# Two graph layers on one core: a block's degrees taken behind the new group's fields instead of ahead of them

## The chip, the cores and the metric

One Trainium2 chip, one of its cores. The metric is the device time of one execution of the whole kernel, in microseconds (us); lower is better. Stated times are medians over runs.

## What is computed

There are 6250 nodes with 128 features and 206250 directed edges `src -> dst`, sorted by `dst`, each with a type of nine. The reference, cut to what matters (`segsum` adds the rows of the edges that share an index):

```
h   = relu(layernorm(x))
deg = segsum(1, src)                                  # edges that leave a node
h   = relu(segsum((h * max(deg,1)**-0.5)[src], dst))  # first layer
x   = x + h @ W0.T + b0
h   = relu(layernorm(x))
m   = segsum(h[src] @ Wmsg.T + bmsg + embed[type], dst)   # second layer
x   = x + GRU(m, h)
```

The edge list holds every edge in both directions and one loop at each node, so the edges that leave a node are as many as those that reach it. The kernel counts the arriving ones, by type.

## The kernel before

The nodes stand in 49 blocks of 128. The kernel turns the edge list into a dense matrix of edge counts ("adjacency") and then does both layers as matrix products.

*Prologue* (the stage of the change). The edge list is turned and written to a DRAM table `flat`; for each pair of nodes the row of `flat` in which its edges begin is searched (`row_i`). Then a loop of seven passes, `for i in range(NCH)`, goes over seven groups of pairs (six of 4 x 125 pairs, one of 125). Three closures do the work:

- `fetch` gathers a group's edges from `flat` by up to four indirect DMAs on GpSimd's queue (L650) into `got`, which has two buffers. VectorE compares the edges with the pairs (L665, two instructions) and multiplies the comparison into the fields (L672, two). TensorE turns the fields with up to 36 small products (L681). ScalarE copies the three results out of PSUM: `typ` (L691), `code_t` and `lo_t` (L694).
- `count` counts a group's edges by type: five masks on VectorE (`m_dve`, L706), four on ScalarE (`m_act`, L709), nine products and one more on TensorE (L710, L711), two copies on ScalarE into `counts` (L713).
- `degrees` adds up the counts of seven blocks, 896 nodes: seven tiny products on TensorE (L720) into `deg`, which has one PSUM buffer; VectorE makes `scale` out of `deg` (L728) and copies it into `reach` (L731); ScalarE takes the square root of `scale` (L732). The first L732 is preceded by the load of a table for the root.

Then come `rows_of` (reciprocal of the root, L742; shift, L743; seven scaled blocks, L759, on ScalarE as L757 for the last three) and `terms_of` (the float32 rows split into two parts for the products, L763 and L764), which make one of seven pieces of the table `tab1`. In pass i the loop fetches group i, counts group i-1 and makes table piece i-3. Behind the loop the last degrees, counts and rows follow, with the first one-hot tiles (L353).

In the prologue VectorE's instructions stand in the order in which the code issues them (`tc.manual_schedule(engines={DVE})`). The order on TensorE, ScalarE and GpSimd is made by the scheduler; SP's too. Each engine works off its own list in order, so an instruction that waits holds up all that stands behind it.

*First layer.* One-hot tiles are made by VectorE (L353), multiplied on TensorE into adjacency columns (L843), copied out by ScalarE (L855), widened (L947), and multiplied with `tab1` (L811). The adjacency goes to DRAM. *Second layer.* It is read back (L1007), widened by ScalarE (L1011) or VectorE (L1018) and multiplied with the second table; then the GRU (L1061 to L1096). A general path behind a run-time test is not taken for this data.

Of the kernel before, what the change touches and what calls it, by code (L numbers as in the profile page):

```python
# [272 lines left out]
def by_matrix(  # L273
# [117 lines left out]
    with tc.tile_pool(name="pro", bufs=1) as pro, tc.manual_schedule(engines={mybir.EngineType.DVE}):  # L391
# [251 lines left out]
        groups = [(b, min(GB, WB - b)) for b in range(0, WB, GB)]  # L643
        typ_of = {}

        def fetch(b0_, nb):

            got = wnd.tile([P, GB, ROWS, 4, HALF], I16, name="got")
            for b in range(nb):
                nc.gpsimd.indirect_dma_start(  # L650
                    out=got[:, b].rearrange("p r f j -> p (r f j)"),
                    out_offset=None,
                    in_=edges_flat,
                    in_offset=bass.IndirectOffsetOnAxis(ap=row_i[:, b0_ + b : b0_ + b + 1], axis=0),
                )
            typ_of[b0_] = wnd.tile([P, GB * WP], BF16, name="typ")
            w0_ = b0_ * WP
            turns_ = {i: pps.tile([P, 4, P], F32, name="turn") for i in (1, 0, 2)}
            n = nb * ROWS
            g = got[:, :nb].rearrange("p b r f j -> p (b r) f j")  # L660
            inside = first_place[:, 2 * NB * (P - 6) - 2 * GB * ROWS * HALF : 2 * NB * (P - 6)]
            inside = inside.rearrange("p (d a j) -> p d a j", d=2, j=HALF)
            fields = wnd.tile([P, GB * ROWS, 3, 2, HALF], BF16, name="fields")
            for d in range(2):
                nc.vector.tensor_tensor(  # L665
                    inside[:, d, :n].rearrange("p a (j t) -> p a j t", t=2),
                    g[:, :, 0, :].rearrange("p a (j t) -> p a j t", t=2),
                    mine[d][:, b0_ * ROWS : b0_ * ROWS + n].unsqueeze(2).to_broadcast([P, n, HALF // 2, 2]),
                    ALU.is_equal,
                )  # L670
            for d in range(2):
                nc.vector.tensor_tensor(  # L672
                    fields[:, :n, :, d, :],
                    g[:, :, 1:, :],
                    inside[:, d, :n].unsqueeze(2).to_broadcast([P, n, 3, HALF]),
                    ALU.mult,
                )
            for i in (1, 0, 2):
                for b in range(nb):
                    for r in range(ROWS):  # L680
                        nc.tensor.matmul(  # L681
                            turns_[i][:, b, :],
                            fields[:, b * ROWS + r, i].rearrange("p d j -> p (d j)"),
                            ident_b,
                            start=(r == 0),
                            stop=(r == ROWS - 1),
                        )
            for i in (1, 0, 2):
                ws = turns_[i][:, :nb, :WP]
                if i == 1:  # L690
                    nc.scalar.copy(typ_of[b0_][:, : nb * WP].rearrange("j (b p) -> j b p", p=WP), ws)  # L691
                else:
                    to = (code_t, None, lo_t)[i][:, w0_ : w0_ + nb * WP, :]
                    nc.scalar.copy(  # L694
                        to.rearrange("j (b p) t -> j b p t", p=WP), ws.unsqueeze(3).to_broadcast([P, nb, WP, 2])
                    )

        def count(b0_, nb):

            n = nb * WP  # L700
            typ = typ_of.pop(b0_)[:, :n]
            sums_t = tps.tile([P, 512], F32, name="sums")
            for k in range(TYPES):
                if k < first_level:
                    m = wnd.tile([P, GB * WP], BF16, name="m_dve", bufs=6)
                    nc.vector.tensor_scalar(m[:, :n], typ, float(1 + k), None, op0=ALU.is_equal)  # L706
                else:
                    m = wnd.tile([P, GB * WP], BF16, name="m_act", bufs=4)
                    nc.scalar.activation(m[:, :n], typ, AF.Sign, bias=levels[:, k - first_level : k - first_level + 1])  # L709
                nc.tensor.matmul(sums_t[:both, :n], sel[:, k, :], m[:, :n], start=(k == 0), stop=False)  # L710
            nc.tensor.matmul(sums_t[:both, :n], top, ones_b[:1, :n], start=False, stop=True)  # L711
            for d in (0, 1):
                nc.scalar.copy(counts[:, b0_ * WP : b0_ * WP + n, d], sums_t[32 * d : 32 * d + rows3, :n])  # L713

        def degrees(c):
            blocks = slice(c * CB, (c + 1) * CB)
            deg = dps.tile([P, CB], F32, name="deg")
            for k in range(CB):
                w = (c * CB + k) * P // 2
                nc.tensor.matmul(  # L720
                    deg[:, k : k + 1],
                    counts[:TYPES, w : w + P // 2, :].rearrange("t w d -> t (w d)"),
                    ones_b[:, :1],
                    start=True,
                    stop=True,
                )

            nc.vector.scalar_tensor_tensor(  # L728
                scale[:, blocks], deg, 1.0, dev[:, blocks], op0=ALU.max, op1=ALU.mult
            )  # L730
            nc.vector.tensor_copy(reach[:, blocks], deg)  # L731
            nc.scalar.activation(scale[:, blocks], scale[:, blocks], AF.Sqrt)  # L732
# [6 lines left out]
        def rows_of(c):  # L739

            blocks = slice(c * CB, (c + 1) * CB)
            nc.vector.reciprocal(scale[:, blocks], scale[:, blocks])  # L742
            nc.vector.scalar_tensor_tensor(  # L743
                shift_[:, blocks], mean[:, blocks], -0.5, scale[:, blocks], op0=ALU.mult, op1=ALU.mult
            )
            if c < NCH - 2:
                f_of[c] = wnd.tile([P, CB, H], F32, name="f1", bufs=1)
            else:

                place = wnd.tile([P, GB * ROWS, 3, 2, HALF], BF16, name="fields")  # L750
                place = place.rearrange("p a f d j -> p (a f d j)")[:, : 2 * CB * H]
                f_of[c] = place.bitcast(F32).rearrange("p (b f) -> p b f", f=H)
            for k in range(CB):
                b = c * CB + k
                to, of, by, add = f_of[c][:, k, :], xs[:, b, :], scale[:, b : b + 1], shift_[:, b : b + 1]
                if c >= NCH - 3:
                    nc.scalar.activation(to, of, AF.Identity, bias=add, scale=by)  # L757
                else:
                    nc.vector.tensor_scalar(to, of, by, add, op0=ALU.mult, op1=ALU.add)  # L759

        def terms_of(c):
            f, tab = f_of.pop(c), tab1[c]
            nc.vector.tensor_scalar(tab[:, 0], f, 0.0, None, op0=ALU.max)  # L763
            nc.vector.scalar_tensor_tensor(  # L764
                tab[:, 1], f, 0.0, tab[:, 0].bitcast(F32), op0=ALU.max, op1=ALU.subtract
            )

        for i in range(NCH):
            if i >= 3:
                degrees(i - 3)  # L770
            fetch(*groups[i])
            if i >= 1:
                count(*groups[i - 1])
            if i >= 3:
                rows_of(i - 3)
                terms_of(i - 3)
# [366 lines left out]
def gnn_kernel(tc, *args):  # L1143
    with tc.tile_pool(name="bad", bufs=1) as pool:
        bad_i = pool.tile([P, 1], I32, name="bad_i")
        by_matrix(tc, bad_i, *args)
        general(tc, bad_i, *args)
# [47 lines left out]
```

## Time and profile before

| | |
|---|---|
| median of 3 runs | 931.22 us (930.29 to 931.83) |
| the profiled execution | 934.99 us |
| its span, first to last instruction | 933.20 us |
| granted TensorE clock over the span | 0.96 of full |
| TensorE busy | 852.5 us, 91% |
| VectorE busy | 799.1 us, 86% |
| ScalarE busy | 712.3 us, 76% |
| GpSimd busy | 54.6 us, 6% |
| first fetch issued on GpSimd | 31.27 us |
| first fields on VectorE (L665) | 38.58 us |
| first one-hot tile (L353) | 97.28 us |
| first adjacency products that go on without a break (L843) | 113.56 us |

Times of instructions count from the span's start. A timeline row has the start, the time taken, engine, line, operation, output and input with their shapes, how many instructions were merged into the row, and in brackets the engine's idle time before it with what ended it. A row of waits has the waiter, what it waited for, the sum, the number of times and the longest. Ends of TensorE's instructions are modelled, and consecutive instructions of an engine overlap a little, so starts are the safer readings.

### The profile page before, as it was taken

How to read it: one execution, taken by the hardware profiler on the slowest of the kernel's cores; microseconds unless marked ns; L12 is line 12 of the kernel's file. 1: busy time of each engine (PE TensorE's matmuls, PEld its weight loads, DVE VectorE, ACT ScalarE, POOL GpSimd, SP SyncE). 2: the span in 40 equal slices, each digit the busy share in tenths (PEclk: the TensorE clock that was granted, in tenths of full speed). 3: DMA queues.
4: the chain of work that ended last, by engine and by line, in shares of the span. 5: the costliest groups of instructions: out<-in, count | busy, mean ns of one | idle time of the engine just before them, and what ended most of it. 6: DMA issues, size and time to landing. Idle time of an engine off the chain costs nothing.

```text
span 933.2 us, 24704 instructions
## 1 busy us (share of the span) xinstructions
PE 852.5 (91%) x10859; PEld 717.7 (77%) x10859; DVE 799.1 (86%) x835; ACT 712.3 (76%) x1205; POOL 54.6 (6%) x103
## 2 busy tenths in 40 slices
PE   3566499999998999999999979999999999999995
PEld 3354399998997999899999979776777777777775
DVE  5869999999999999999999768998888888877754
ACT  2277898999898899899999984776667676675752
POOL 4561000000000000000000000000000000000000
PEclk9579699999999999999999989999999999999998
DMA  9430177787787689678688798776777667766640
GB/s 283 126 105 32 40 185 238 221 264 232 221 263 233 186 250 276 191 235 273 203 244 274 216 313 289 257 267 211 279 281 243 234 239 264 266 216 225 212 128 23
DMA packets 205664, 203.72 MB, mean 218 GB/s; under 512 B 11178, under 2 KB 190881, under 8 KB 205393
## 3 DMA queue, kind: packets, MB, share of 16 engines
q1 hardware_dynamic: 198904, 173.34, 60.5%
q0 software_dynamic: 6032, 27.43, 7.9%
q8 instruction: 86, 1.41, 0.6%
q10 hardware_dynamic: 612, 1.30, 0.4%
q14 instruction: 30, 0.25, 0.1%
HBM read 95.68 MB, written 83.87 MB: 192 GB/s over the span
## 4 chain that ended last, share of the span: by engine, by line
PE 64%; ACT 14%; DVE 10%; issue 6%; DMA 4%; POOL 1%; another core or an unknown queue 0%; DVEq 0%; SPq 0%; ACTq 0%; POOLq 0%
PE acc L811 45%; ACT adj L855 8%; PE ev L843 7%; DMA piece<-adj_d 3%; ACT wide L947 3%; PE gate L1073 3%; PE gate L1061 3%; DVE wide L1018 2%; PE acc L876 2%; DVE leave L999 1%; PE turn L681 1%; DVE fields L672 1%; ACT f L1030 1%; PE sums L710 1%; DVE hot_l L353 1%
## 5 line engine op out<-in xcount | busy, mean ns | idle before, releaser
L811 PE MATMUL acc<-wide,tab 128*128 128x256 f32 (+2 forms) x3374 | 580.9, 327 | 4.3 <-issue 2.2
L811 PEld LDWEIGHTS acc<-wide,tab 128*128 128x128 f32 x3374 | 489.5, 189 | 65.6 <-issue 13.6
L855 ACT CAST adj<-ev 128x1960 bf16<-128x1960 f32 (+2 forms) x221 | 282.5, 1340 | 35.9 <-PE ev L843 19.9
L1011 ACT ACTIVATE wide<-piece 128x512 fp32r<-128x512 bf16 (+1 forms) x336 | 200.9, 601 | 63.5 <-issue 33.9
L353 DVE TENSOR_TENSOR hot_l<-lo_t,iota 128x3840 bf16<-128x3840 bf16 (+2 forms) x109 | 223.4, 2050 | 5.8 <-PE ev L843 5.7
L999 DVE TENSOR_REDUCE leave<-piece 128x7 f32<-128x3584 bf16 (+2 forms) x43 | 154.9, 3602 | 23.5 <-DMA piece<-adj_d 23.4
L947 ACT CAST wide<-adj 128x1792 fp32r<-128x1792 bf16 (+1 forms) x75 | 126.2, 1682 | 0.0
L843 PE MATMUL ev<-hot_c,hot_l 64*128 64x49 bf16 x6204 | 100.7, 182 | 7.1 <-DVE hot_c L353 3.6
L843 PEld LDWEIGHTS <-hot_l 64*128 64x128 bf16 x6204 | 88.5, 93 | 21.8 <-issue 4.4
L353 DVE TENSOR_TENSOR hot_c<-code_t,iota 128x1500 bf16<-128x1500 bf16 (+2 forms) x109 | 97.4, 893 | 0.0
L1018 DVE CAST wide<-piece 128x3584 fp32r<-128x3584 bf16 (+2 forms) x43 | 82.5, 1920 | 12.3 <-PE acc L811 12.3
L947 DVE CAST wide<-adj 128x1792 fp32r<-128x1792 bf16 (+1 forms) x75 | 80.5, 1087 | 14.4 <-ACT adj L855 13.6
L1011 ACT ACTIVATION_READ_ACCUMULATOR wide<-piece 128x1 f32 x336 | 63.2, 188 | 0.0
L1066 ACT COPY sum_sb<-acc 128x512 f32<-128x512 f32 (+2 forms) x13 | 7.3, 563 | 58.4 <-PE acc L811 58.4
L811 PE MATMUL acc<-wide_last,tab 128*128 128x256 f32 x350 | 48.2, 283 | 0.0
L811 PEld LDWEIGHTS acc<-wide_last,tab 128*128 128x128 f32 x350 | 43.6, 188 | 0.4
L943 POOL DMA_DIRECT2D wide_last<-adj x25 | 13.7, 550 | 447.4 <-PE acc L811 207.9
L1073 PE MATMUL gate<-sum_sb,wsum_sb 128*128 128x512 f32 (+2 forms) x78 | 35.0, 585 | 0.1
L1061 PE MATMUL gate<-hT,whh_sb 128*128 128x512 f32 (+2 forms) x78 | 33.7, 567 | 0.0
L681 PE MATMUL turn<-ident_b,fields 128*128 128x128 bf16 x225 | 20.6, 275 | 13.7 <-DVE fields L672 10.3
L681 PEld LDWEIGHTS <-fields 128*128 128x128 bf16 x225 | 19.0, 128 | 15.8 <-DVE fields L672 12.1
L650 POOL DMA_INDIRECT got<-flat,row_i x25 | 27.4, 1098 | 14.7 <-DVE m_dve L706 7.7
(167 smaller groups left out, 504.4 us busy)
## 6 DMA issues: line engine op xcount, KB each, us to landing
adj_d<-adj SPq DMA_DIRECT2D x24, 3136.0 KB
piece<-adj_d SPq DMA_DIRECT2D x77, 896.0 KB
wide_last<-adj POOLq DMA_DIRECT2D x24, 896.0 KB
piece<-adj_d SPq DMA_DIRECT2D x14, 672.0 KB
piece<-adj_d SPq DMA_DIRECT2D x7, 448.0 KB
out_dram<-res SPq DMA_DIRECT2D x11, 256.0 KB
xs<-in_x_dram SPq DMA_DIRECT2D x6, 448.0 KB
adj_d<-adj SPq DMA_DIRECT2D x1, 1568.0 KB
```

Source lines behind the costliest of these rows:

```text
L353: nc.vector.tensor_tensor(to.rearrange("p j (k t) -> p j k t", t=2), twice.unsqueeze(2).to_broadcast([P, n, m // 2, 2]), of[:, :m].rearran ...
L650: nc.gpsimd.indirect_dma_start(out=got[:, b].rearrange("p r f j -> p (r f j)"), out_offset=None, in_=edges_flat, in_offset=bass.IndirectOf ...
L681: nc.tensor.matmul(turns_[i][:, b, :], fields[:, b * ROWS + r, i].rearrange("p d j -> p (d j)"), ident_b, start=(r == 0), stop=(r == ROWS ...
L811: nc.tensor.matmul(acc[:, : 2 * P].rearrange("f (t n) -> f t n", t=2) if twice else acc[:, :nd], tab[:, s, i, :], a[:, i, :P].unsqueeze(1) ...
L843: nc.tensor.matmul(ps[:, d % banks, slot * NB : (slot + 1) * NB], hot_l[half, t + d // 2, :], hot_c[half, t + d // 2, :NB], start=True, st ...
L855: nc.scalar.copy(adjs[c][:, :, at : at + n].rearrange("p n (j d) -> p n j d", d=banks), ps[:, :banks, : n // banks * NB].rearrange("p d (j ...
L947: make(wides[c][q][:, :, :n], a)
L999: nc.vector.tensor_reduce(leave[:, q * HP : (q + 1) * HP, c], piece, AX.X, ALU.add)
L1011: nc.scalar.activation(pieces[q][:, i, :nd], piece[:, i, :nd], AF.Copy, accum_out=leave[:, q * HP + i, c : c + 1],)
L1018: nc.vector.tensor_copy(pieces[q][:, :, :nd], piece[:, :, :nd])
L1061: nc.tensor.matmul(ps[:, :nd], whh_sb[:, g * H : (g + 1) * H], hT[:, :nd], start=True, stop=(g == 2))
L1073: nc.tensor.matmul(ps[:, :nd], wsum_sb[:, g * H : (g + 1) * H], sum_sb[:, :nd], start=False, stop=True)
```

## The change

In the loop over groups the call of `fetch` is put ahead of the call of `degrees`:

```diff
         for i in range(NCH):
+            fetch(*groups[i])
             if i >= 3:
                 degrees(i - 3)
-            fetch(*groups[i])
             if i >= 1:
                 count(*groups[i - 1])
             if i >= 3:
                 rows_of(i - 3)
                 terms_of(i - 3)
```

`degrees` is called in passes 3 to 6 for blocks 0 to 3 (of seven each). On VectorE its two instructions, L728 and L731, then stand behind the four of `fetch` (L665, L672) in these passes; TensorE's, ScalarE's and GpSimd's order is made anew by the scheduler from the new order of the code. The order behind the loop and SP's order stay as they are.

## The prediction

> **What bounds the kernel now.** I read the page first (shares and slices), then VectorE's waits in the stage of the change, then the timelines of VectorE, ScalarE and TensorE over 50 to 115 us. The page:
>
> ```profile
> PE 852.5 (91%) x10859; PEld 717.7 (77%) x10859; DVE 799.1 (86%) x835; ACT 712.3 (76%) x1205; POOL 54.6 (6%) x103
> ...
> PE   3566499999998999999999979999999999999995
> ...
> DVE  5869999999999999999999768998888888877754
> ACT  2277898999898899899999984776667676675752
> ```
>
> A slice is 23.3 us. TensorE is the bound from slice 5 on; the changed loop lies in slices 1 to 4 (about 31 to 97 us), where VectorE is the fullest. TensorE's adjacency stage begins only when the tables of this loop's end are made, so what the loop loses is handed on to the end. VectorE's waits from 36 to 114 us:
>
> ```profile
> DVE scale L728 <- PE deg L720: 5.5, 1, 5.5
> DVE adj L665 <- DMA got<-flat,row_i: 3.1, 1, 3.1
> DVE adj L665 <- issue: 2.6, 2, 1.7
> DVE scale L742 <- ACT scale L732: 1.5, 3, 0.8
> ```
>
> Only the first lies at the moved place: pass i=3 waits 5.5 us for block 0's degrees, with the fields of group 3 queued behind. VectorE's timeline there:
>
> ```profile
> 55.19 2.05 DVE L706 TENSOR_SCALAR m_dve<-typ 128x500 bf16<-128x500 bf16 x5
> 62.76 0.17 DVE L728 SCALAR_TENSOR_TENSOR scale<-deg,dev 128x7 f32<-128x7 f32 x1 [5.52 <-PE deg L720]
> ...
> 62.97 1.03 DVE L665 TENSOR_TENSOR adj<-got,mine 128x768 bf16<-128x768 int16 x2
> 63.91 2.62 DVE L672 TENSOR_TENSOR fields<-got,adj 128x2304 bf16<-128x2304 int16 x2
> 66.45 1.09 DVE L706 TENSOR_SCALAR m_dve<-typ 128x500 bf16<-128x500 bf16 x5
> 67.44 0.20 DVE L742 RECIPROCAL scale<-scale 128x7 f32<-128x7 f32 x1
> ```
>
> TensorE (the degrees of block 0; `turn` at half clock, at full clock, at half clock):
>
> ```profile
> 62.24 0.32 PE L720 MATMUL deg<-ones_b,counts 9*128 9x1 bf16 x7
> ...
> 66.59 4.02 PE L681 MATMUL turn<-ident_b,fields 128*128 128x128 bf16 x36 [0.91 <-DVE fields L672]
> ...
> 75.63 2.18 PE L681 MATMUL turn<-ident_b,fields 128*128 128x128 bf16 x36
> ...
> 83.86 3.50 PE L681 MATMUL turn<-ident_b,fields 128*128 128x128 bf16 x36 [1.61 <-DVE fields L672]
> ```
>
> ScalarE:
>
> ```profile
> 63.87 1.41 ACT L713 CAST counts<-sums 27x500 bf16<-27x500 f32 x2
> 65.30 1.28 ACT L732 ACT_TABLE_LOAD   x1
> 66.59 0.21 ACT L732 ACTIVATE scale<-scale 128x7 f32<-128x7 f32 x1
> ...
> 76.64 0.58 ACT L691 CAST typ<-turn 128x500 bf16<-128x500 f32 x1
> 77.18 0.99 ACT L694 CAST code_t<-turn 128x1000 bf16<-128x1000 f32 x1
> 78.07 1.00 ACT L694 CAST lo_t<-turn 128x1000 bf16<-128x1000 f32 x1
> ...
> 90.33 1.41 ACT L713 CAST counts<-sums 27x500 bf16<-27x500 f32 x2
> 91.61 0.19 ACT L732 ACTIVATE scale<-scale 128x7 f32<-128x7 f32 x1
> ```
>
> See in it that the square root of block 0 is done at 66.80, 0.64 us before the reciprocal wants it. That 0.64 is all the slack it has.
>
> **The change part by part.** No instruction is added or removed. On VectorE L728 and L731 go behind L665 and L672 in passes 3 to 6. Only VectorE's order is written by hand here; the scheduler puts TensorE, ScalarE and GpSimd in order, and it moves more: on ScalarE the square roots of blocks 0 and 3 (L732; block 0's with the table load) come to stand behind the three copies `typ`, `code_t`, `lo_t` of the new group, where they stood ahead of them; those of blocks 1 and 2 go behind two `m_act` masks.
>
> *Pass 3, VectorE.* L706 ends at 57.24. Group 3's last gather is issued at 53.85; group 2's landed 3.1 us behind its issue (48.56 to 51.70), so group 3 is there by 57.0. Fields start at 57.2 and take 3.48 (62.97 to 66.45): done at 60.7. The degrees come from TensorE at 62.74 as before, since its order up to them (L681, L710, L720) is the same: 2.0 of the 5.5 us stay. The masks L706 then end at 64.0, 3.4 us sooner than at 67.44.
>
> *Pass 3, ScalarE.* What VectorE wants next is the root. ScalarE reaches 65.28 (end of `counts`) as before. Now come the three copies, 76.64 to 79.07 in the trace, 2.43 us: the table load starts at 67.7, and with 1.29 and 0.21 the root is done at 69.2; reciprocal at 69.23 against 67.44, **+1.8**. This needs the `turn` of group 3 in time: TensorE can start it at 62.74. At full clock (75.63: first third after 0.86, the others 0.67 each) it is done by 64.9, ahead of ScalarE. At half clock the trace's third copy came 5.2 us behind the start (66.59, `lo_t` at 71.83): that gives 68.0, and +3.0. I take +1.8, because TensorE is now busy without a break from 55.3 and the clock had been granted full at 60.6.
>
> *The page that speaks against it.* The Trainium skill, "ScalarE: Activation LUTs", section "What ACT_TABLE_LOAD costs", has a switch at about 2.66 us: 1.28 of load and a drain of 1.38. The trace has the load at 65.30 behind an end at 65.28 and the root at 66.59: 1.29, no drain. Before, it lay in VectorE's shadow; now it is on the path. By the page the reciprocal would be at +3.2; I take the trace, +1.8.
>
> *Passes 4 and 5.* From the reciprocal to the next fields was 4.17 (67.44 to 71.61); L728 and L731 with 0.14 have left it: fields at 73.26, **+1.65**. Then VectorE has no wait before (8.64 a pass: 71.61, 80.25, 88.88) and none now: L728 of pass 4 at 76.7, its root at 77.0, the reciprocal due at 77.9; pass 5 alike. Cover: 0.9 us; gone, each us late costs one.
>
> *Pass 6.* Fields of group 5 end at 85.4; its `turn` takes 2.1 or 3.4 (75.63 and 83.86 to the next L710): 87.5 or 88.8. In the trace `counts` of group 4 ended 4.31 behind that (87.30 to 91.61): 91.8 or 93.1. Ahead of block 3's root now stand a mask and group 6's three copies, 1.40 (91.71 to 93.11), and itself 0.19: 93.4 or 94.7. The reciprocal was at 91.84, so **+1.6 or +2.9**; middle 2.2, since the clock at that time can go either way.
>
> *From there.* The same chain, and the wait of 0.2 at 96.81 goes, since ScalarE has its masks behind it: about **+2.0** at the first adjacency products (113.56).
>
> *The clock at the hand-over.* In the trace TensorE runs at half clock from 113.56 until 118.60. Were the grant to come at the same time, 2.0 us less of work would be done at half speed and 1.0 be given back. The skill's "TensorE: Matmul & The Clock Gate", "Part 1: The HAM clock gate", calls the window free-running, so that cold counts vary from run to run; by that nothing is given back on average. Trace: +1.0; page: +2.0. I take +2.0 and keep +1.0 in the range.
>
> *Other queues.* GpSimd: the third `terms` copy (L778) goes behind group 5's four gathers, which now start at 61.0 (when group 3's fields are done) and not at 66.81; the copy comes at about 66 instead of 61.65. Four small stores on SP's queue wait for it, and the next there is `types_d`, due when the last counts end at 98.40: 30 us of cover. The gathers themselves come earlier; nobody waits for them. TensorE: block 1's seven `deg` matmuls (0.3 us) move into group 2's sums, beside a wait for masks: nothing.
>
> **Sum.** +2.0 on the profiled execution's 934.99 (span 933.20 and 1.79 around it) is 937.0. The median of the runs shown is 931.22, 3.8 below that execution; the loss is the same: **933.2**.
>
> **The rivals.**
> - *The loss is hidden*: the clock pays half back and pass 6 runs at full clock (+1.6 - 0.2, halved: 0.7): 931.9. For it: grant at 118.60. Against it: it needs both.
> - *Faster*: VectorE keeps the 3.4 us won in pass 3 and the denser TensorE stays at full clock: 927.8 to 929. It would need block 0's root ahead of group 3's copies; ScalarE's order speaks against it.
> - *Slower by more*: half clock in both places, +3.0 and another 1.3 in pass 6, or a drain at the table load: 935.0 to 936.
>
> That the change doesn't do what it says can't be: VectorE's order has the move in all passes.
>
> **How the numbers follow.** A measurement of this kernel tells 0.2% (1.9 us) from no change. Likeliest case, +1.0 to +2.9: 0.45, of it 0.33 above 1.9. Hidden: 0.30, nearly all within (0.28, with 0.02 slower). Slower by more: 0.17. Faster: 0.08. Slower 0.33 + 0.02 + 0.17 = 0.52; same 0.12 + 0.28 = 0.40; faster 0.08. Range: from 930.4 (hidden, with the runs' own 0.8 below) to 936.2 (half clock twice); outside lie the faster case and some of the slowest.
>
> **What would show it.** Right: L728 of pass 3 still at 62.8 with a wait of 2 us; a new wait of about 5 us at the first L742, ended by ScalarE's L732, that reciprocal near 69.2; fields of group 4 near 73.3; about 1.5 us of wait at pass 6's L742; first adjacency products near 115.5. Wrong: the first reciprocal at or before 67.4, no wait on L732, or a hand-over within 0.5 us of 113.56.

## The result, and the profile after

The changed kernel took 932.35 us (median of 20 runs), the kernel before 930.47 us (20 runs beside it): ratio 1.0020, 95% interval [1.0011, 1.0029], a loss of 1.9 us. The profiled execution of the changed kernel took 932.71 us (span 930.8), so it lies at its own median; that of the kernel before took 934.99, 4.5 us above its median. The two profiles are therefore read for who waits for whom. Their spans are not subtracted.

The page of the changed kernel: busy time, then the tenths of 40 slices.

```profile
PE 848.6 (91%) x10859; PEld 713.4 (77%) x10859; DVE 799.4 (86%) x835; ACT 712.2 (77%) x1205; POOL 54.3 (6%) x103
...
PE   3466499999999999999999979999999999999995
...
DVE  5879999999998999999999778988888888877753
```

Busy times are those of before to within 0.6 per cent, and the counts are the same: the change is one of order alone. VectorE's waits in 36 to 116 us (who waited, for whom, us in total, times, longest):

```profile
DVE scale L742 <- ACT scale L732: 5.0, 3, 3.7
DVE adj L665 <- issue: 2.7, 2, 1.8
DVE adj L665 <- DMA got<-flat,row_i: 1.9, 1, 1.9
DVE tab L763 <- ACT fields L757: 0.2, 1, 0.2
```

The wait for the degrees (L728, 5.5 us before) is gone, and the wait for ScalarE's root has grown from 1.5 to 5.0 us, with 3.7 of it in one piece. VectorE's timeline shows where (start, duration, instruction, idle time before it and its releaser):

```profile
55.69 1.02 DVE L665 TENSOR_TENSOR adj<-got,mine 128x768 bf16<-128x768 int16 x2
56.62 2.62 DVE L672 TENSOR_TENSOR fields<-got,adj 128x2304 bf16<-128x2304 int16 x2
59.16 0.15 DVE L728 SCALAR_TENSOR_TENSOR scale<-deg,dev 128x7 f32<-128x7 f32 x1
...
59.31 1.26 DVE L706 TENSOR_SCALAR m_dve<-typ 128x500 bf16<-128x500 bf16 x5
64.28 0.20 DVE L742 RECIPROCAL scale<-scale 128x7 f32<-128x7 f32 x1 [3.72 <-ACT scale L732]
...
68.49 1.02 DVE L665 TENSOR_TENSOR adj<-got,mine 128x768 bf16<-128x768 int16 x2
...
88.56 0.20 DVE L742 RECIPROCAL scale<-scale 128x7 f32<-128x7 f32 x1 [0.52 <-ACT scale L732]
```

Fields stand ahead of degrees, and the degrees were there when L728 came; VectorE then stands still in front of its first reciprocal. ScalarE at the same time:

```profile
58.84 1.42 ACT L713 CAST counts<-sums 27x500 bf16<-27x500 f32 x2
60.28 0.58 ACT L691 CAST typ<-turn 128x500 bf16<-128x500 f32 x1
60.85 0.99 ACT L694 CAST code_t<-turn 128x1000 bf16<-128x1000 f32 x1
61.74 1.00 ACT L694 CAST lo_t<-turn 128x1000 bf16<-128x1000 f32 x1
62.75 1.28 ACT L732 ACT_TABLE_LOAD   x1
64.05 0.21 ACT L732 ACTIVATE scale<-scale 128x7 f32<-128x7 f32 x1
```

Three copies of the new group, 2.47 us from 60.28 to 62.75, now lie between the counts and the root. TensorE had the `turn` of this group without a break and at full clock:

```profile
59.30 2.18 PE L681 MATMUL turn<-ident_b,fields 128*128 128x128 bf16 x36 [0.67 <-DVE fields L672]
```

### The profile page after: what moved, and what is told of

Read it like the earlier page. It is cut to its first block, busy times and chain, and to the rows that moved or that the text cites. A ratio compares the mean times of both kernels' runs of the same rounds, so it can differ in the third digit from the quotient of the medians.

```text
span 930.8 us, 24705 instructions
## 1 busy us (share of the span) xinstructions
PE 848.6 (91%) x10859; PEld 713.4 (77%) x10859; DVE 799.4 (86%) x835; ACT 712.2 (77%) x1205; POOL 54.3 (6%) x103
## 4 chain that ended last, share of the span: by engine, by line
PE 65%; ACT 14%; DVE 11%; issue 5%; DMA 3%; POOL 1%; DVEq 0%; SPq 0%; ACTq 0%; POOLq 0%
PE acc L811 48%; ACT adj L855 8%; PE ev L843 7%; PE gate L1061 3%; PE gate L1073 3%; ACT wide L947 2%; DMA piece<-adj_d 2%; PE acc L876 2%; DVE wide L1018 1%; DVE hot_l L353 1%; DVE fields L672 1%; POOL got L650 1%; ACT f L1030 1%; DVE leave L999 1%; DMA dst_i<-in_dst_dram 1%
## 5 line engine op out<-in xcount | busy, mean ns | idle before, releaser
L353 DVE TENSOR_TENSOR hot_l<-lo_t,iota 128x3840 bf16<-128x3840 bf16 (+2 forms) x109 | 223.3, 2049 | 7.1 <-PE ev L843 6.9
L353 DVE TENSOR_TENSOR hot_c<-code_t,iota 128x1500 bf16<-128x1500 bf16 (+2 forms) x109 | 97.2, 892 | 0.0
L681 PE MATMUL turn<-ident_b,fields 128*128 128x128 bf16 x225 | 17.3, 248 | 20.1 <-DVE fields L672 20.1
L681 PEld LDWEIGHTS <-fields 128*128 128x128 bf16 x225 | 16.0, 113 | 22.6 <-DVE fields L672 22.6
```

Source lines behind the costliest of these rows:

```text
L353: nc.vector.tensor_tensor(to.rearrange("p j (k t) -> p j k t", t=2), twice.unsqueeze(2).to_broadcast([P, n, m // 2, 2]), of[:, :m].rearran ...
L681: nc.tensor.matmul(turns_[i][:, b, :], fields[:, b * ROWS + r, i].rearrange("p d j -> p (d j)"), ident_b, start=(r == 0), stop=(r == ROWS ...
```

## The experiments

First theory: the root behind the copies costs the time in pass 3. Its rivals: the table load, now on the path, costs it; or the other passes do. This first theory is "theory A" in the expectations of e1 to e8. After e1 to e4 a further one was added: TensorE's results come late while gathers are under way, and the root behind the copies hands this on to VectorE. It is "theory D" in e5 to e7 and "theory A" in f1 to f4, where its rival B gives that lateness another cause. Each ratio is against the kernel before on the same chip in the same group of runs; its median there was 932.93 us (first group, e1 to e4), 932.46 (second, e5 to e8) and 931.82 (third, f1 to f4). Reciprocal and hand-over are from each run's one profile: start of the first L742, and of the third one-hot build (L353; the second stands under the name `adj`), behind which TensorE's adjacency products run on. From there to the end every one of these profiles has 819.5 to 824 us.

| run | edit | ratio, 95% interval | first reciprocal | hand-over |
|---|---|---|---|---|
| before | | 1 | 67.44 | 110.49 |
| changed | | 1.0020 [1.0011, 1.0029] | 64.28 | 107.16 |
| e1 | roots ahead of the copies | 1.0010 [0.9991, 1.0030] | 65.32 | 108.51 |
| e2 | table loaded early | 1.0057 [1.0037, 1.0078] | 69.96 | 113.07 |
| e3 | both | 1.0012 [0.9998, 1.0026] | 68.66 | 112.25 |
| e4 | pass 3 alone | 1.0061 [1.0037, 1.0086] | 73.07 | 116.58 |
| e5 | changed, again | 1.0047 [1.0027, 1.0066] | 71.65 | 114.93 |
| e6 | pass 6 alone | 1.0028 [1.0014, 1.0041] | 66.85 | 110.25 |
| e7 | passes 4 and 5 alone | 1.0034 [1.0022, 1.0046] | 66.56 | 111.09 |
| e8 | before, table loaded early | 1.0007 [0.9992, 1.0021] | 70.67 | 113.71 |
| f1 | changed, a third time | 1.0085 [1.0063, 1.0107] | 72.31 | 116.71 |
| f2 | gathers of group 5 held | 1.0045 [1.0032, 1.0057] | 69.17 | 112.47 |
| f3 | of groups 4 and 5 held | 1.0074 [1.0052, 1.0095] | 67.92 | 115.57 |
| f4 | e1, group 5 held | 1.0011 [0.9996, 1.0025] | 65.16 | 107.91 |

**e1, roots ahead of the copies.** `fetch` is cut ahead of its copies, so that VectorE keeps the changed order, and ScalarE's roots of blocks 0 and 3 go back ahead of the copies:

```
+            turns_of[b0_] = turns_
+
+        def copies(b0_, nb):
+
+            turns_ = turns_of.pop(b0_)
+            w0_ = b0_ * WP
             for i in (1, 0, 2):
                 ws = turns_[i][:, :nb, :WP]
                 ...
         for i in range(NCH):
             fetch(*groups[i])
             if i >= 3:
                 degrees(i - 3)
+            copies(*groups[i])
```

> VectorE's order is that of the changed kernel; the three copies typ, code_t, lo_t of the new group are issued in the code behind degrees, so on ScalarE the square roots of blocks 0 and 3 stand ahead of them again. Theory A (the loss is ScalarE's order: the root behind the copies): the loss goes; the first reciprocal comes within 0.3 us of where the root is done, with table load about 1.6 us behind the end of counts; 930.0, ratio to before 0.9985 to 1.0005. Theory B (the loss is VectorE's own order: the degrees' two instructions behind the fields): as the changed kernel, ratio 1.002.

Measured 1.0010. The root no longer waits for the copies; its last late copy comes behind it (line numbers are 7 higher here than in the changed kernel; "remote" means that the trace names no instruction that ended the wait):

```profile
63.78 1.28 ACT L739 ACT_TABLE_LOAD   x1
65.08 0.21 ACT L739 ACTIVATE scale<-scale 128x7 f32<-128x7 f32 x1
...
68.42 0.99 ACT L701 CAST lo_t<-turn 128x1000 bf16<-128x1000 f32 x1 [1.64 <-remote]
```

That `lo_t`, of group 3, came 7.7 us behind its turn's start. In the changed kernel's order the root would have stood behind it. The gain that was expected did not come: VectorE still waits 3.1 us at its first reciprocal.

**e2 and e3, the table load.** A root of `eps` ahead of the loop loads the table in the prologue; e2 is the changed kernel with it, e3 is e1 with it, and e8 below the kernel before with it:

```
+        nothing = pro.tile([P, 1], F32, name="nothing")
+        nc.scalar.activation(nothing, eps, AF.Sqrt)
```

> The changed kernel with one dummy root on ScalarE at its start, so that the table is loaded there and not ahead of block 0's root. Theory A: the load lies on the path of pass 3, so 1.28 us less of wait at the first reciprocal (3.7 to about 2.4); ratio to before about 1.001. Theory B (VectorE's order): no change against the changed kernel, ratio 1.002.

> Both edits: root ahead of the copies, table loaded at the start. Theory A: VectorE keeps part of what it won in pass 3; the first reciprocal waits less than 1 us, 1.5 to 2 us sooner than in before; 928.7, ratio 0.998. Theory B: ratio 1.002.

e2 1.0057, e3 1.0012. Neither lies where the first theory had it. On the same chip e3 is level with e1, and e2 still loses 5 us without its 1.28 us of load: the load is not the term that decides. The root's place is: e2 and e3 differ in it alone, by 4.1 us of their medians, and their intervals do not overlap. ScalarE in e2 (line numbers 2 higher):

```profile
68.83 0.99 ACT L696 CAST lo_t<-turn 128x1000 bf16<-128x1000 f32 x1 [1.90 <-remote]
69.72 0.21 ACT L734 ACTIVATE scale<-scale 128x7 f32<-128x7 f32 x1
```

The root follows `lo_t` at once, and `lo_t` was late. VectorE had waited 7.2 us.

**e4, e6, e7, parts of the loop alone** (set against the kernel before; here e4).

```
         for i in range(NCH):
-            if i >= 3:
+            if i >= 3 and i not in (3,):      # e6: (6,)   e7: (4, 5)
                 degrees(i - 3)
             fetch(*groups[i])
+            if i in (3,):
+                degrees(i - 3)
```

> fetch ahead of degrees in pass 3 alone; passes 4 to 6 as in before. Theory A as recorded: pass 3 loses 1.65 and hands it on, pass 6 adds nothing of its own: ratio 1.0013, with a wait of 3 to 5 us at the first reciprocal and the wait at pass 6's reciprocal as before (about 0.8). Theory C (pass 3 only trades one wait for another, and the loss is pass 6's): ratio 1.000.

> fetch ahead of degrees in pass 6 alone. Theory A as recorded: block 3's root behind one mask and three copies, 1.4 us later than before, of which the wait of 0.8 at that reciprocal grows to about 2: ratio 1.0010 to 1.0015. Theory D: no gathers are under way in pass 6, the tail's waits absorb it: ratio 1.000.

> fetch ahead of degrees in passes 4 and 5 alone. Theories A and D: VectorE has no wait there before or after (cover 0.9 us at each reciprocal): ratio 1.000, no wait at L728 or L742 of passes 4 and 5.

e4 1.0061, e6 1.0028, e7 1.0034. None of the three lies where it was expected. Every part alone loses, and together (0.6 + 0.3 + 0.3%) they exceed the whole of any group, so they are no shares of it. In the whole, pass 3's wait gives the later passes slack: VectorE's reciprocals in the changed kernel's profile stand 8.8 and 8.6 us apart in passes 3 to 5 (8.64 before), with no wait. That this is why the parts do not add up is a reading, not shown. In e7's profile pass 4's reciprocal waits 0.95 us for the root, and pass 6's L728 1.37 us for degrees; from the first reciprocal to pass 6's it takes 26.2 us (24.4 before). Where e6's loss arises its profile does not show: pass 6's reciprocal waits 0.94 us, against 0.80 before. In e4 both waits are paid, for the degrees and for the root:

```profile
67.28 0.17 DVE L728 SCALAR_TENSOR_TENSOR scale<-deg,dev 128x7 f32<-128x7 f32 x1 [7.67 <-remote]
...
73.07 0.20 DVE L742 RECIPROCAL scale<-scale 128x7 f32<-128x7 f32 x1 [4.55 <-ACT scale L732]
```

**e5, the changed kernel again, and e8, the kernel before with an early load.**

> The changed kernel unaltered, beside the variants on one chip. Theory A as recorded: ratio 1.002. Theory D (TensorE stalls while gathers are under way, and pass 3 now starts its products into the gathers of group 5, so the loss is larger where the stalls are): ratio 1.004 to 1.006, as for pass 3 alone, and a wait of more than 6 us in sum at the first L728 and L742 in the trace.

> The kernel before with one dummy root at ScalarE's start, so that the table load of 1.28 us leaves pass 3. Theory A: block 0's root had 0.64 us of slack there, so nothing: ratio 1.000. Rival: the early load itself costs or the load was on the path: ratio off 1 by more than 0.0015.

e5 1.0047, e8 1.0007. e5 lies where theory D had it, and e8 where the first theory had it: without the change the load costs nothing that can be measured. VectorE's wait for the root in e5 is more than twice that of the first profile:

```profile
DVE scale L742 <- ACT scale L732: 10.8, 5, 9.1
```

TensorE's rows do not show why. By them the turn of group 3 ran without a gap and ended at 63.39, and yet ScalarE's third copy was held until 69.11:

```profile
61.21 2.18 PE L681 MATMUL turn<-ident_b,fields 128*128 128x128 bf16 x36
69.11 0.99 ACT L694 CAST lo_t<-turn 128x1000 bf16<-128x1000 f32 x1 [3.05 <-remote]
```

The trace also keeps the time of each semaphore update, by which an engine tells the others that a result is there. TensorE's stand at 62.52 and 64.78, and then eight of them between 69.08 and 69.32, within 0.24 us. In the rows such products end 0.21 us apart, so most of them had run before; what came late is the signal.

**f1 to f4, gathers held back.** Ahead of the gathers of group 5 (f2, f4) or of groups 4 and 5 (f3) GpSimd copies four elements a partition of group 3's `lo_t` into their buffer:

```
             got = wnd.tile([P, GB, ROWS, 4, HALF], I16, name="got")
+            if b0_ == 5 * GB:
+                late = lo_t[:, 3 * GB * WP : 3 * GB * WP + GB, 0]
+                nc.gpsimd.tensor_copy(got[:, :, 0, 0, 0], late)
```

> The changed kernel unaltered, beside the three that follow on the same chip. Expected 1.002 to 1.005 against the kernel before, and in the profile a wait of VectorE at the first reciprocal (L742) of 4 to 9 us, ended by ScalarE's root.

> The changed kernel, but the gathers of group 5 are held back until ScalarE has copied lo_t of group 3 (a GpSimd copy of 4 elements a partition from lo_t into the buffer ahead of the gathers). Theory A (TensorE's results come late while GpSimd's gathers are under way, and the root behind the copies hands that on to VectorE): turn of group 3 meets only the tail of group 4's gathers, so the lo_t copy of group 3 starts 2.4 to 5 us behind the turn's first product instead of 5 to 8, VectorE's wait at the first reciprocal falls to 3 to 5 us, and the ratio to the kernel before to 1.000 to 1.003. Theory B (only ScalarE's order counts, and the lateness of the turn has another cause): the wait and the ratio are those of the unaltered changed kernel within 0.001, 6 to 9 us where that has them.

> The changed kernel, with the gathers of groups 4 and 5 both held back until ScalarE has copied lo_t of group 3, so that no gather is under way in the turn of group 3. Theory A: the lo_t copy starts 2.4 us (full clock) to 4.1 us (half clock) behind the turn's first product, VectorE's wait at the first reciprocal is 3 to 4.5 us, no longer; against this the fields of group 4 wait for their gathers, some 2 to 4 us, so the ratio is 1.001 to 1.005. Theory B: the lo_t copy still starts 5 to 8 us behind the turn's start.

> VectorE's order as in the changed kernel, the roots of blocks 0 and 3 ahead of the copies on ScalarE, and group 5's gathers held back until lo_t of group 3 is copied. Theory A: with the root ahead VectorE does not wait for the turn, so the hold brings little: 0.998 to 1.001, at best the one version that is level with or just below the kernel before. Theory B: 1.000 to 1.002, as without the hold.

The changed kernel as it is came to 1.0085 here, more than was expected. Its TensorE in the `turn` of group 3 (f1):

```profile
61.80 1.14 PE L681 MATMUL turn<-ident_b,fields 128*128 128x128 bf16 x15
63.33 0.22 PE L681 MATMUL turn<-ident_b,fields 128*128 128x128 bf16 x1 [0.39 <-issue]
64.06 0.33 PE L681 MATMUL turn<-ident_b,fields 128*128 128x128 bf16 x3 [0.52 <-issue]
65.46 0.38 PE L681 MATMUL turn<-ident_b,fields 128*128 128x128 bf16 x4 [1.07 <-issue]
66.91 1.55 PE L681 MATMUL turn<-ident_b,fields 128*128 128x128 bf16 x13 [1.07 <-issue]
```

36 products take 6.7 us, with idle time that no wait in the trace explains. GpSimd issues group 5's gathers from 60.5 to 65.2 us. Three of the four gaps end when signals of TensorE get out: its semaphore updates stand at 64.02, 65.45 and 66.91, the rows go on at 64.06, 65.46 and 66.91. No instructions were being fetched meanwhile: the trace has no such transfer from 61.8 to 68.4. In f2, with these gathers held until 68.2, the same 36 products (line numbers 3 higher):

```profile
61.88 2.18 PE L684 MATMUL turn<-ident_b,fields 128*128 128x128 bf16 x36
```

They run without a gap, as they do in f3 (60.62, 2.18 us) and f4 (61.34, 2.18 us). That alone would prove little, since they do so in e1, e2 and e5 too, without a hold. But now the signals keep step: in f2 the three parts of the turn end at 62.72, 63.39 and 64.06 by the rows and are signalled at 62.74, 63.41 and 64.08. From the turn's start to the third copy it takes 4.7 us in f2 and f3 and 5.2 in f4, and ScalarE does not wait for TensorE there; in the six versions e1 to e5 and f1, with `fetch` ahead in pass 3 and no hold, it takes 7.4 to 8.4 (2.4 in the first profile of the changed kernel). VectorE in f1:

```profile
67.02 0.17 DVE L728 SCALAR_TENSOR_TENSOR scale<-deg,dev 128x7 f32<-128x7 f32 x1 [7.63 <-remote]
72.31 0.20 DVE L742 RECIPROCAL scale<-scale 128x7 f32<-128x7 f32 x1 [4.07 <-ACT scale L732]
```

and in f2:

```profile
61.98 0.17 DVE L731 SCALAR_TENSOR_TENSOR scale<-deg,dev 128x7 f32<-128x7 f32 x1 [2.60 <-PE deg L723]
69.17 0.20 DVE L745 RECIPROCAL scale<-scale 128x7 f32<-128x7 f32 x1 [5.96 <-ACT scale L735]
```

f2's first reciprocal comes 3.1 us sooner than f1's, and the ratio falls from 1.0085 to 1.0045, or 3.7 us; the intervals do not overlap. So holding the gathers of group 5 removes the lateness here, as theory A has it, and rival B, for which nothing would change, is refuted. The gain is not where theory A put it: the wait at the first reciprocal does not fall to 3 to 5 us but grows, from 4.1 to 6.0, while the wait for the degrees falls from 7.6 to 2.6. The ratio stays above the 1.003 that was expected at most. In f2 ScalarE reached group 2's `lo_t` only at 61.72 (56.74 in the first profile of the changed kernel), because the turns of groups 1 and 2 had been late under earlier gathers, 8.3 and 7.8 us to their `lo_t`. f3 leaves group 3's turn free of gathers altogether and has the earlier reciprocal (67.92), but its wait there is 6.0 us as well (3 to 4.5 expected), and it pays the hold with a wait of 2.96 us for group 4's fields. Its 1.0074 is above what was expected:

```profile
74.98 1.03 DVE L668 TENSOR_TENSOR adj<-got,mine 128x768 bf16<-128x768 int16 x2 [2.96 <-DMA got<-flat,row_i]
```

f4 has the root ahead of the copies and lies at 1.0011, where e1 and e3 lie without the hold; that does not tell its two theories apart. On this chip that is 7 us less than f1, and its first reciprocal is 7.15 us sooner. It differs from f2 by the root's place alone: 3.3 us of their medians, and again the intervals do not overlap. None of the versions beats the kernel before; e1, e3 and f4 cannot be told from it.

## Why the prediction was right

The predicted time was 933.2 us and the measured one 932.35; the predicted loss 2.0 us and the measured one 1.9. The mechanism stands: the root comes to stand behind three copies, and VectorE waits for it. The pairs e2 and e3, f2 and f4 show it: with VectorE's order kept and the root put back, each comes down to 1.0012 or 1.0011. The rival "faster" asked for just that, and even then nothing is gained; why not is open. That predicted and measured loss agree to 0.1 us is luck: the terms of the sum were off by more than that, and in the two other groups of runs the same kernel lost 4.0 and 8.5 us of the median. Of the signs that the prediction named, the new wait on L732 came. A sign of being wrong came too: in the profile the first reciprocal is at 64.28, ahead of 67.4, and the first adjacency products are at 110.22, not near 115.5. Signs of this kind were badly chosen: they take the times of one profile for fixed, and the degrees came 3.6 us sooner in this one. By the prediction's steps:

- *Pass 3, VectorE* (2.0 of the 5.5 us of wait stay, L728 at 62.8): in the profile none stayed, L728 ran at 59.16. The degrees were there sooner, since TensorE and ScalarE had lost less in groups 1 and 2 than in the profile of before. In f1 the wait was 7.63 us. The step took one profile's time of the degrees for a fixed one; it moves by about 8 us between profiles.
- *Pass 3, ScalarE* (+1.8): order right, copies 2.47 us against the 2.43 of the sum, and the wait 3.7 us for the "about 5". As a size it fails: the sum put `turn` at 2.2 us at full clock or 4.0 at half, and the third copy at most 5.2 us behind its start. With gathers under way it came 7.9 us behind in e5 and in f1, and the wait reached 9.1 us in e5.
- *Table load* (1.29 by the trace, not the 2.66 of the Trainium skill, "ScalarE: Activation LUTs", section "What ACT_TABLE_LOAD costs"): here 62.75 to 64.05, 1.30 us, with no drain. The trace's number held.
- *Passes 4 and 5* (cover 0.9 us): no wait there in the first profile of the changed kernel, 0.72 us at pass 5 in e5. As e7 shows, the cover is thin: alone, pass 4 waits 0.95 us.
- *Pass 6* (+1.6 or +2.9, wait about 1.5): wait 0.52, and the first to the last reciprocal of the four takes 24.3 us, as before (24.4). In this profile it adds next to nothing; in f1 the wait is 1.79 and the four take 25.7.
- *Other queues*, "the gathers themselves come earlier; nobody waits for them": this is the step that failed, though the number came out. Nobody waits for them, but they now run beside block 0's degrees and group 3's `turn`, which f2 shows to cost 3.7 us on that chip. In the kernel before, group 5's gathers (66.8 to 70.8) also fell into that turn, which took 5.24 us to `lo_t`; but the root was already through, so nothing on VectorE stood behind it.
- *Clock at the hand-over* (nothing given back): no run separates it. TensorE's half clock there lasts about 5.0 us in the profile of before (113.56 to 118.6) and about 3.5 in that of the changed kernel (110.22 to 113.7), but from the hand-over to the end all the profiles are spread over 4.5 us.

The forecast was met on the chip of the result. The same kernel came to 1.0047 and 1.0085 in the other two groups, and the interval of the last lies wholly above that of the result. A reading, not shown, is that about 2 us is the loss where TensorE is little disturbed, and that what the sum leaves out comes on top. What sets its amount, which the kernel before does not show in its own medians (930.5 to 932.9 us), is open.

## What to carry to other kernels

When an order written by hand is changed on one engine, look at what the scheduler does with the others: here VectorE won its wait back and lost it again because a small root fell behind three copies on ScalarE. A short operation on the way between two busy engines goes ahead of bulk copies, and then it is also safe from whatever delays these: here its place was worth 4.1 us (e2 against e3) and 3.3 us (f2 against f4). Before a term is costed from one profile, look in other stages or runs for how far its duration moves.

## What the runs showed of the hardware

TensorE's signals can be held up while GpSimd's indirect gathers are under way. From a turn's first product to the start of the third copy it took 2.4 to 3.9 us in group 5, where no gather was in flight in any run. In groups 1 to 3 with gathers in flight it took 4.1 to 8.8 us, 10.7 and 11.9 in e8, and 2.4 to 2.9 in the first profile of the changed kernel alone. Part of this is ScalarE's own lag, and half clock, at which 36 products took 4.02 us instead of 2.18.

What the held signals look like stands in the semaphore updates between 36 and 100 us. In 13 of the 14 profiles TensorE has 3 to 19 updates that follow the one before within 50 ns, and each time a gather had been issued within the 4.3 us before. In the other profile no two are closer than 0.17 us. ScalarE and VectorE have none in any profile. TensorE's own issue can stop with it (f1, gaps that end as signals get out) or run on (e5, 2.18 us whole, the third copy 7.9 us behind). With the gathers held back group 3's turn was signalled without a bunch in f2, f3 and f4.

Gathers are not enough by themselves: in the first profile of the changed kernel they were in flight, and no signal was held. What ties the two together was not found.
